# A graph layer with top-p attention: one guard less, and the finished tile's root moved behind the guess's chain on GpSimd

## The chip, the cores and the metric

The kernel runs on one core of a Trainium2 chip. Its time is in device microseconds, the median of several runs; of the kernel before, three runs gave 1342.86, 1344.52 and 1345.33 us. A profile is one execution more, taken with the hardware profiler; its rows have times from the start of the span. TensorE appears in it as PE (matmuls and transposes) and PEld (weight loads), VectorE as DVE, ScalarE as ACT, GpSimd as POOL, SyncE (which issues most DMAs) as SP.

## The reference

3327 nodes with 256 features, a sparse weighted adjacency `S`, and two steps of a mix of diffusion and attention. All is float32.

```python
h = relu(layernorm(x))                       # X of the layer
R = S + eye; R = R / R.sum(-1)               # diffusion
for n in range(2):
    q = Xa @ W1.T @ W2.T; k = Xa @ W3.T      # 64 wide
    probs = softmax(q @ k.T)                 # 3327 x 3327
    # top-p: keep the largest probabilities until their sum reaches 0.9, drop the rest
    A = probs * mask; A = A / max(A.sum(-1), 1e-12)
    Xf = R @ Xf
    Xa = A @ Xa
    Z = Z + Xf @ U1[n].T + Xa @ U2[n].T
out = x + (layernorm(h + Z) * ln_g + ln_b)
```

The sort of the reference is not done. Of each row only one number is wanted: the smallest probability that is kept.

## The kernel before, in words

Rows are tiled by 128: 26 tiles (`NT`), the last one partly filled, and 3328 columns (`NP`). The program makes two passes over the tiles, **step 0** (about the first 740 us) and **step 1** (the rest). In each, a tile goes through the same stations, spread over neighbouring iterations of one loop:

- `weights`: TensorE makes the logits `q @ k.T` in four pieces (`pl`, L597), ScalarE takes their exponentials into the row block `e` (L601; the last piece L607 and L609), with their sum `Z`.
- `measured`: a guess at the threshold. ScalarE computes a first guess from moments of the logits, and two or three times runs over the whole 128 x 3328 block (L632) to sum or count what lies below a guess; between these passes stand chains of operations on one column (128 x 1), the columns of the small tile `g`. They are done on ScalarE, VectorE and GpSimd. In step 1 (`measured_twice`) the last of these chains is the one the change touches: VectorE makes the mass below the second guess (L698, L699) and a slope (L705, L706); ScalarE takes logarithms (L701 to L703); GpSimd makes the exponent (L707 to L711); ScalarE's L713 turns it into the guess proper, `col(16)`. The passes read the block, the columns come from their sums `oa`.
- `settle`: VectorE keeps the elements below the guess (L728, 128 x 3328), takes the 8 largest of each of 20 segments (L733), of these the 32 or 40 largest (L740, L742), finds among them the exact threshold, and masks the row block with it (L762, 128 x 3328; L759 for the first and the last tile, in two pieces).
- `Sums`: TensorE transposes the masked block (`pt`, L808), ScalarE copies the transposes out (`eT`, L810), and TensorE sums `A @ X` (`pa`, L822).
- `spread`: diffusion by gathering rows (L899, L920: indirect DMAs that GpSimd issues) and small matmuls (`pr`, L928).
- `finish` (step 1): L958 adds attention and diffusion, L461 and L462 take mean and variance, `inverse` on GpSimd makes 1/sqrt of the variance, the **root** (L468 adds the epsilon, L469 is the power), L966 makes minus mean times root, and L973 to L976 scale, shift and add the input rows `xr`, all on GpSimd.

At the end a proof checks that every row's threshold was among the candidates. If one row fails, a second, complete program (`search_graph_layer`) runs behind the first. **Guards** protect the guess: where it cannot be trusted, a huge number is added, so that all elements become candidates. One guard goes by count (fewer than some 15 or 30 elements lie above), one by mass (too little lies below).

The order of work is written out by hand. An iteration has seven parts, and a table (`PLAN`, L1141; `OPEN` and `LAST` for the first and last iterations of step 1) names for each part the stations that take one stride, letter by letter: `m` measured, `w` weights, `d` settle, `s` spread, `f` finish, `g` one gather, `c` and `n` the rest of the last iteration's settle and measured. Each engine's queue then stands in the order of this text. In iteration i, `m` works for tile i + 1, and `f` for a tile that was finished in part 3. So on GpSimd, in step 1, between the third and the last part stand: four gathers, L688 to L691 (columns of the second guess), the root of the finished tile with L966, the chain L696 to L711, one gather; then L675 to L677 of the next tile.

Of the kernel before, what the change touches and what calls it, by code (L numbers as in the profile page):

```python
# [9 lines left out]
F32 = mybir.dt.float32  # L10
# [4 lines left out]
ALU = mybir.AluOpType  # L15
# [3 lines left out]
P = 128  # L19
# [4 lines left out]
NP = NT * P  # L24
# [288 lines left out]
BIG = 1.0e30  # L313
LNBIG = 69.0
# [31 lines left out]
def guess_graph_layer(ctx, tc, x, adj, w1t, w2t, w3t, u1t, u2t, ln_g, ln_b, out, flag):  # L346
# [9 lines left out]
    small = ctx.enter_context(tc.tile_pool(name="small", bufs=4))  # L356
# [5 lines left out]
    V, G, S, PE = nc.vector, nc.gpsimd, nc.scalar, nc.tensor  # L362
# [264 lines left out]
    def con(k):  # L627
        return one[:, k : k + 1]
# [5 lines left out]
    def measured_once(r):  # L634
        e, ms = r["e"], r["ms"]


        col = guessed(r, small.tile([P, 17], F32, tag="g", name="g"), 0)
        S.activation(col(4), col(2), AF.Square, bias=con(4))
        S.activation(col(11), col(4), AF.Identity, scale=ms(5), bias=ms(6))  # L640
        S.activation(col(1), col(0), AF.Exp, scale=-1.0, bias=con(5))
        G.tensor_scalar(col(7), col(9), 0.5, None, ALU.mult)
        G.tensor_scalar(col(8), col(9), 0.5 * NP, None, ALU.mult)
        G.tensor_scalar(col(5), col(1), OFFSET[0], None, ALU.mult)
        G.tensor_scalar(col(10), col(9), col(5), 1.0, ALU.mult, ALU.add)
        yield
        oa = small.tile([P, 3], F32, tag="oa", name="oa")
        through(e, AF.Relu, col(9), -1.0, oa[:, 0:1])
        yield
        through(e, AF.Sign, col(9), -1.0, oa[:, 1:2])  # L650
        yield
        S.activation(col(3), oa[:, 0:1], AF.Identity, scale=-1.0, bias=col(8))
        S.activation(col(4), oa[:, 1:2], AF.Relu, scale=col(7), bias=col(3))
        S.activation(col(6), col(4), AF.Ln, scale=col(1), bias=con(2))
        S.activation(col(3), col(4), AF.Square, scale=col(1), bias=con(1))
        S.activation(col(3), col(3), AF.Ln, scale=0.5, bias=col(10))
        S.activation(col(3), col(3), AF.Identity, scale=-1.0, bias=col(6))
        S.activation(col(3), col(3), AF.Exp, scale=col(11))
        yield

        V.tensor_scalar(col(5), oa[:, 1:2], NP - 31.0, BIG, ALU.is_gt, ALU.mult)
        V.tensor_scalar(col(6), col(4), col(1), 0.35, ALU.mult, ALU.is_lt)
        V.scalar_tensor_tensor(col(5), col(6), BIG, col(5), ALU.mult, ALU.add)
        V.tensor_scalar(col(3), col(3), 1.0e20, col(9), ALU.min, ALU.mult)
        V.tensor_tensor(col(16), col(3), col(5), ALU.add)

    def measured_twice(r):
# [4 lines left out]
        col = guessed(r, small.tile([P, 18], F32, tag="g", name="g"), 1)  # L672
# [6 lines left out]
        oa = small.tile([P, 3], F32, tag="oa", name="oa")  # L679
# [13 lines left out]
        through(e, AF.Sign, col(13), -1.0, oa[:, 2:3])  # L693
        yield
        d1 = col(17)
        G.tensor_scalar(col(0), oa[:, 2:3], NP - 61.0, BIG, ALU.is_gt, ALU.mult)  # L696
        G.tensor_scalar(col(0), r["Z"], 0.035, col(0), ALU.mult, ALU.add)
        V.tensor_scalar(col(15), oa[:, 2:3], oa[:, 1:2], col(14), ALU.subtract, ALU.mult)  # L698
        V.tensor_scalar(d1, col(15), col(4), 0.0, ALU.add, ALU.max)  # L699

# [3 lines left out]

        V.tensor_scalar(col(12), col(4), d1, 1.0e-30, ALU.subtract, ALU.add)  # L705
        V.reciprocal(col(12), col(12))  # L706
        G.tensor_scalar(col(12), col(12), col(8), 0.85, ALU.mult, ALU.max)  # L707
        G.tensor_scalar(col(11), col(12), 1.2, col(11), ALU.min, ALU.mult)
        G.tensor_tensor(col(2), col(3), col(2), ALU.subtract)
        G.tensor_scalar(col(15), d1, col(0), LNBIG, ALU.is_lt, ALU.mult)  # L710
        G.tensor_tensor(col(6), col(6), col(15), ALU.add)  # L711
        yield
        S.activation(col(16), col(2), AF.Exp, scale=col(11), bias=col(6))  # L713
        yield
# [242 lines left out]
    def finish(t, y, pa, ra):  # L957
        V.scalar_tensor_tensor(y, pa, ra, y, ALU.mult, ALU.add)  # L958
        yield
        mv = spread_of(y)  # L960
        yield
        xr = row.tile([P, D], F32, tag="xr", name="xr", bufs=1)
        nc.sync.dma_start(xr, x[t * P : (t + 1) * P])
        rstd = inverse(mv)
        nm = small.tile([P, 1], F32, tag="nm", name="nm")
        G.tensor_scalar(nm, mv[:, 0:1], rstd, -1.0, ALU.mult, ALU.mult)  # L966
        yield
        if t == NT - 1:
            G.tensor_tensor(xr, xr, bet, ALU.add)
            V.scalar_tensor_tensor(y, y, mv[:, 0:1], gam, ALU.subtract, ALU.mult)  # L970
            V.scalar_tensor_tensor(y, y, rstd, xr, ALU.mult, ALU.add)
        else:
            G.tensor_scalar(y, y, rstd, nm, ALU.mult, ALU.add)  # L973
            G.tensor_tensor(y, y, gam, ALU.mult)
            G.tensor_tensor(xr, xr, bet, ALU.add)
            G.tensor_tensor(y, y, xr, ALU.add)  # L976
        h = min(P, N - t * P)
        nc.sync.dma_start(out[t * P : t * P + h], y[:h])
# [152 lines left out]
    def refetch(t):  # L1131
# [7 lines left out]


    PLAN = (("gmdsssa", "gmcdsssa", "edawwpg", "gmsdga", "gmspdea", "ohgdawwqg", "gehmgq"),  # L1141
            ("llcmss", "lnms", "lwwnfd", "lcmdsssgggg", "fdsmwqdf", "llmdf", "lmwdg"))

    LAST = {NT - 1: ("cfss", "cn", "nd", "sss", "fddddddsf", "f", ""), NT: ("c", "", "", "ff", "ff", "fv", "f"),
            NT + 1: ("fv", "f", "", "", "f", "f", "f")}
# [142 lines left out]
```

## Time and profile before

| | us |
|---|---|
| median of three runs | 1344.52 |
| profiled execution | 1346.05 |
| its span, first to last instruction | 1344.3 |
| TensorE busy in the span | 1259.3 (94%) |
| VectorE busy | 1151.8 (86%) |
| ScalarE busy | 1074.2 (80%) |
| GpSimd busy | 1017.4 (76%) |

The page has one row of tenths per engine for forty slices of the span. Step 0 fills slices 3 to 21, step 1 slices 23 to 40. A share over the whole span mixes two stages with different limits, so the prediction reads them apart. A row of the order of time gives start, duration, engine, line, operation, what it writes and reads, its shape, and in brackets how long its engine was idle just before and who ended that.

### The profile page before, as it was taken

The page shows a single profiled execution, that of the slowest core. Times are in us where ns is not written, and L with a number is a line of the kernel's source. Part 1 is how long each engine was busy: PE and PEld are TensorE (multiplying, and loading weights), DVE is VectorE, ACT ScalarE, POOL GpSimd, SP SyncE. Part 2 cuts the span into 40 slices and gives each one's busy share as a digit, 9 for nine tenths or more (in the row PEclk, how much of TensorE's full clock was granted, in tenths as well). Part 3 has the DMA queues.
Part 4 walks back from the last instruction along what each step waited for, and adds up shares of the span by engine and source line. Part 5 has one row for each costly group of instructions (what it writes and reads, how often), then busy time and mean ns, then how long its engine had stood idle before and what let it go on. Part 6 is the DMA issues. An engine that isn't in the chain of part 4 may idle for free.

```text
span 1344.3 us, 22106 instructions
## 1 busy us (share of the span) xinstructions
PE 1259.3 (94%) x6396; PEld 956.0 (71%) x6396; DVE 1151.8 (86%) x3481; ACT 1074.2 (80%) x2315; POOL 1017.4 (76%) x1411
## 2 busy tenths in 40 slices
PE   5989899999999999999999589999999999999985
PEld 4535677778777787777777367777777777777774
DVE  6876899999999999999981698888998898988993
ACT  5476798888878888888853889899998999999951
POOL 6214888888888888887883587888888888888852
PEclk9999999999999999999999789999999999999998
DMA  7744455454555555455433213132222223131200
GB/s 265 254 132 133 123 153 160 141 157 136 144 157 145 154 142 155 137 152 154 117 103 91 79 50 90 54 95 62 86 79 69 87 65 95 53 95 61 82 24 23
DMA packets 100723, 153.13 MB, mean 114 GB/s; under 512 B 16849, under 2 KB 67152, under 8 KB 100592
## 3 DMA queue, kind: packets, MB, share of 16 engines
q1 hardware_dynamic: 83056, 108.72, 25.5%
q0 software_dynamic: 16640, 42.69, 12.7%
q8 instruction: 53, 0.87, 0.3%
q14 instruction: 78, 0.64, 0.2%
q10 hardware_dynamic: 896, 0.21, 0.1%
HBM read 120.88 MB, written 27.28 MB: 110 GB/s over the span
## 4 chain that ended last, share of the span: by engine, by line
PE 52%; ACT 25%; POOL 10%; DVE 7%; issue 3%; DMA 0%; SPq 0%; DVEq 0%; POOLq 0%; ACTq 0%
PE pa L822 23%; ACT ja L632 14%; PE pl L597 7%; PE pt L808 6%; PE pr L928 5%; PE pz L947 3%; PE pz L1016 3%; POOL g L710 3%; ACT eT L810 3%; ACT e L601 2%; POOL xg L920 2%; DVE cand L733 1%; ACT x L601 1%; DVE bb L740 1%; POOL g L707 1%
## 5 line engine op out<-in xcount | busy, mean ns | idle before, releaser
L822 PE MATMUL pa<-xw,eT 128*128 128x256 f32 x1352 | 323.7, 384 | 4.0 <-DVE s L958 3.8
L632 ACT ACTIVATE ja<-e,g 128x3328 uint8<-128x3328 f32 x106 | 325.7, 3073 | 0.1
L822 PE MATMUL pa<-x,eT 128*128 128x256 f32 x1352 | 322.0, 379 | 0.0
L822 PEld LDWEIGHTS pa<-xw,eT 128*128 128x128 f32 x1352 | 250.7, 190 | 64.0 <-issue 20.9
L822 PEld LDWEIGHTS pa<-x,eT 128*128 128x128 f32 x1352 | 242.8, 190 | 25.5
L733 DVE MAX8 cand<-w 128x8 f32<-128x168 f32 (+1 forms) x1040 | 253.4, 317 | 0.0
L810 ACT COPY eT<-pt 128x512 f32<-128x512 f32 (+1 forms) x364 | 198.4, 553 | 45.4 <-PE pt L808 39.1
L899 POOL DMA_INDIRECT ac<-in_adj,index x130 | 188.2, 1448 | 60.1 <-issue 26.5
L920 POOL DMA_INDIRECT xg<-bx,index x130 | 184.4, 1419 | 48.6 <-issue 16.2
L808 PE MATMUL pt<-ident,e 128*128 128x128 f32 x1144 | 176.0, 276 | 17.1 <-DVE e L759 8.5
L920 POOL DMA_INDIRECT xg<-vx,index x130 | 164.3, 1264 | 34.0 <-issue 32.9
L808 PEld LDWEIGHTS pt<-ident,e 128*128 128x128 f32 x1144 | 138.8, 143 | 71.0 <-issue 44.1
L728 DVE SCALAR_TENSOR_TENSOR w<-e,g 128x3328 f32<-128x3328 f32 x44 | 164.4, 3737 | 9.1 <-ACT g L713 8.2
L928 PE MATMUL pr<-xg,ac 128*128 128x257 f32 (+1 forms) x520 | 141.5, 396 | 10.4 <-DVE s L1124 7.0
L762 DVE SCALAR_TENSOR_TENSOR e<-e,rec 128x3328 f32<-128x3328 f32 x40 | 147.2, 3680 | 0.6
L601 ACT ACTIVATE e<-pl 128x832 f32<-128x832 f32 x132 | 113.9, 865 | 27.7 <-PE pl L597 24.5
L928 PEld LDWEIGHTS pr<-xg,ac 128*128 128x128 f32 x520 | 93.8, 194 | 37.5 <-issue 14.6
L597 PE MATMUL pl<-both,qT 64*128 64x416 f32 x416 | 100.0, 545 | 7.7 <-ACT e L601 4.3
L597 PE MATMUL pl<-after,qT 64*128 64x416 f32 x416 | 95.9, 555 | 1.8 <-ACT e L601 1.4
L852 DVE TENSOR_REDUCE fm<-at 128x4 f32<-128x512 f32 (+1 forms) x133 | 84.3, 634 | 0.0
L740 DVE MAX8 bb<-cand 128x8 f32<-128x160 f32 x234 | 75.6, 323 | 4.6
L632 ACT ACTIVATE ja<-x,g 128x3328 uint8<-128x3328 f32 x24 | 73.7, 3069 | 0.0
(261 smaller groups left out, 2045.3 us busy)
## 6 DMA issues: line engine op xcount, KB each, us to landing
at<-in_adj SPq DMA_DIRECT2D x114, 256.0 KB
cx<-ac SPq DMA_DIRECT2D x26, 384.0 KB
ac<-cx SPq DMA_DIRECT2D x26, 384.0 KB
wide<-in_adj SPq DMA_DIRECT2D x8, 832.0 KB
e<-in_adj SPq DMA_DIRECT2D x6, 832.0 KB
own<-bx SPq DMA_DIRECT2D x26, 128.5 KB
x<-in_x SPq DMA_DIRECT2D x13, 256.0 KB
qT<-both SPq DMA_DIRECT2D x104, 32.0 KB
```

What stands on the lines that cost most here:

```text
L597: PE.matmul(pl[:, a, :wd], qT[p, :], keys_of(step, a).rearrange("p a b -> p (a b)")[:, c : c + wd], start=True, stop=True)
L601: S.activation(e.rearrange("p (a n) -> p a n", a=2)[:, :, c : c + wd], pl[:, :, :wd], AF.Exp, accum_out=za[:, n : n + 1])
L632: S.activation(ja, e, f, bias=guess, scale=sign, accum_out=total)
L728: V.scalar_tensor_tensor(w, e, col(16), e, ALU.is_lt, ALU.mult, accum_out=d2)
L733: V.max(cand[:, 8 * s : 8 * s + 8], w[:, s * SEG : min(NP, (s + 1) * SEG)])
L762: V.scalar_tensor_tensor(e, e, at(1), e, ALU.is_ge, ALU.mult, accum_out=ra)
L808: PE.transpose(pt[:, j, :], e[:, (j0 + j) * P : (j0 + j + 1) * P], ident)
L810: S.copy(eT[:, :w, :], pt[:, :w, :])
L822: PE.matmul(self.pa, eT[:, c - 4 * k, :], self.xa[:, j, :], start=c == 0, stop=c == NT - 1)
L899: G.indirect_dma_start(out=ac[:, k, :], out_offset=None, in_=rows, in_offset=bass.IndirectOffsetOnAxis(ap=index[:, t, k : k + 1], axis=0), ...
L920: G.indirect_dma_start(out=xg[:, k, :w], out_offset=None, in_=rows, in_offset=bass.IndirectOffsetOnAxis(ap=index[:, t, k : k + 1], axis=0))
L928: PE.matmul(pr[:, :w], ac[:, k, :], own if k == KT - 1 else xg[:, k, :w], start=k == 0, stop=k == KT - 1)
```

## The change

Four edits.

1. In step 0 the guard by mass goes: two VectorE instructions a tile (L662, L663).
2. In step 1 the guard by mass goes too. Two GpSimd operations ahead of the chain (L696, L697) and two at its end (L710, L711) go; the guard by count is now added to the exponent's shift `col(6)` by two operations that stand between VectorE's L706 and L707, and need neither L706 nor ScalarE's logarithms.
3. In `finish` L966 goes; the scaling subtracts the mean and multiplies by the root in one instruction of the same shape.
4. In the table of step 1, part 4 and part 6 run `w` before `m` (logits' exponential before the guess's), and the third stride of `f` (the root, and the load of `xr`) moves from the end of part 5 to part 6, behind `m`. `OPEN` and `LAST` stay.

```diff
@@ measured_once @@
         V.tensor_scalar(col(5), oa[:, 1:2], NP - 31.0, BIG, ALU.is_gt, ALU.mult)
-        V.tensor_scalar(col(6), col(4), col(1), 0.35, ALU.mult, ALU.is_lt)
-        V.scalar_tensor_tensor(col(5), col(6), BIG, col(5), ALU.mult, ALU.add)
         V.tensor_scalar(col(3), col(3), 1.0e20, col(9), ALU.min, ALU.mult)
@@ measured_twice @@
         d1 = col(17)
-        G.tensor_scalar(col(0), oa[:, 2:3], NP - 61.0, BIG, ALU.is_gt, ALU.mult)
-        G.tensor_scalar(col(0), r["Z"], 0.035, col(0), ALU.mult, ALU.add)
...
         V.reciprocal(col(12), col(12))
+        G.tensor_scalar(col(0), oa[:, 2:3], NP - 61.0, LNBIG, ALU.is_gt, ALU.mult)
+        G.tensor_tensor(col(6), col(6), col(0), ALU.add)
         G.tensor_scalar(col(12), col(12), col(8), 0.85, ALU.mult, ALU.max)
         G.tensor_scalar(col(11), col(12), 1.2, col(11), ALU.min, ALU.mult)
         G.tensor_tensor(col(2), col(3), col(2), ALU.subtract)
-        G.tensor_scalar(col(15), d1, col(0), LNBIG, ALU.is_lt, ALU.mult)
-        G.tensor_tensor(col(6), col(6), col(15), ALU.add)
         yield
         S.activation(col(16), col(2), AF.Exp, scale=col(11), bias=col(6))
@@ finish @@
         rstd = inverse(mv)
-        nm = small.tile([P, 1], F32, tag="nm", name="nm")
-        G.tensor_scalar(nm, mv[:, 0:1], rstd, -1.0, ALU.mult, ALU.mult)
...
-            G.tensor_scalar(y, y, rstd, nm, ALU.mult, ALU.add)
+            G.tensor_scalar(y, y, mv[:, 0:1], rstd, ALU.subtract, ALU.mult)
@@ PLAN, step 1 @@
-            ("llcmss", "lnms", "lwwnfd", "lcmdsssgggg", "fdsmwqdf", "llmdf", "lmwdg"))
+            ("llcmss", "lnms", "lwwnfd", "lcmdsssgggg", "fdswmqdf", "llmd", "lwmfdg"))
```

GpSimd's queue in a middle tile of step 1, from the second guess's columns to the gather of part 6 (`g` is the tile of columns, `oa` the sums of the passes, `mv` mean and variance, `rstd` the root). Before:

```order
L691 TENSOR_SCALAR g<-g 128x1
L468 TENSOR_SCALAR rstd<-mv 128x1
L469 TENSOR_TENSOR rstd<-rstd,half 128x1
L966 TENSOR_SCALAR nm<-mv,rstd 128x1
L696 TENSOR_SCALAR g<-oa 128x1
L697 TENSOR_SCALAR g<-rec,g 128x1
L707 TENSOR_SCALAR g<-g 128x1
L708 TENSOR_SCALAR g<-g 128x1
L709 TENSOR_TENSOR g<-g 128x1
L710 TENSOR_SCALAR g<-g 128x1
L711 TENSOR_TENSOR g<-g 128x1
L920 DMA xg<-vx,index 128x256
```

And now; line numbers are those of the changed kernel, in which L705, L706 and L707 are the former L707, L708 and L709:

```order
L689 TENSOR_SCALAR g<-g 128x1
L703 TENSOR_SCALAR g<-oa 128x1
L704 TENSOR_TENSOR g<-g 128x1
L705 TENSOR_SCALAR g<-g 128x1
L706 TENSOR_SCALAR g<-g 128x1
L707 TENSOR_TENSOR g<-g 128x1
L468 TENSOR_SCALAR rstd<-mv 128x1
L469 TENSOR_TENSOR rstd<-rstd,half 128x1
L916 DMA xg<-vx,index 128x256
```

The root has moved from before the chain to behind it, ahead of the gather; three instructions a tile are gone.

ScalarE's queue in the same tile, from the pass over the block in part 3 to part 6 (`eT` are copies of transposes, `e` the row block, `za` the sums). Before:

```order
L810 COPY eT<-pt 128x512
L686 ACTIVATE g<-g,one 128x1
L687 ACTIVATE g<-g 128x1
L601 ACTIVATE e_99,za<-pl 128x2x416
L810 COPY eT<-pt 128x512
L632 ACTIVATE ja,oa<-e_102,g 128x3328
L810 COPY eT<-pt 128x512
L701 ACTIVATE g<-g,one 128x1
L702 ACTIVATE g<-g 128x1
L703 ACTIVATE g<-g,one 128x1
L607 ACTIVATE e_99,za<-pl 128x2x415
L609 ACTIVATE e_99,za<-pl 128x1
```

And now (L684 and L685 are the former L686 and L687; L697 to L699 the former L701 to L703; L806 the former L810):

```order
L806 COPY eT<-pt 128x512
L601 ACTIVATE e_99,za<-pl 128x2x416
L684 ACTIVATE g<-g,one 128x1
L685 ACTIVATE g<-g 128x1
L806 COPY eT<-pt 128x512
L632 ACTIVATE ja,oa<-e_102,g 128x3328
L806 COPY eT<-pt 128x512
L607 ACTIVATE e_99,za<-pl 128x2x415
L609 ACTIVATE e_99,za<-pl 128x1
L697 ACTIVATE g<-g,one 128x1
L698 ACTIVATE g<-g 128x1
L699 ACTIVATE g<-g,one 128x1
```

In part 4 the exponential of the third piece of logits, in part 6 that of the last piece (L607, L609) come before the guess's columns. The queues of TensorE and SyncE keep their order.

## The prediction

> **What bounds the kernel now.** I read the page first, then the busy times by stretch, then who waits for whom, then the order of time in two neighbouring tiles.
>
> From the page, the span and TensorE's busy tenths:
>
> ```profile
> span 1344.3 us, 22106 instructions
> ...
> PE   5989899999999999999999589999999999999985
> ```
>
> From the busy times by stretch (PE, PEld, DVE, ACT, POOL, then clock, DMA share, GB/s): 200 us of step 0, then two neighbouring tiles of step 1.
>
> ```profile
> 300.00:500.00 200.00, 199.88 (x1057) 155.62 (x1056) 189.38 (x574) 167.04 (x415) 167.69 (x192) 1.00 0.52 147
> ...
> 1039.59:1061.89 22.30, 21.19 (x110) 16.31 (x109) 20.64 (x59) 19.95 (x39) 19.77 (x26) 1.00 0.25 75
> 1061.89:1082.43 20.54, 20.48 (x106) 15.76 (x104) 17.96 (x54) 19.87 (x39) 17.74 (x27) 1.00 0.25 80
> ```
>
> Step 0 is TensorE's: 199.88 of 200 us. Step 1 alternates: a tile of 22.30 us, one of 20.54. ScalarE does the same work in both, so the long one holds a wait. From the waits of step 1 (us in total, times, longest):
>
> ```profile
> ACT g L713 <- POOL g L711: 21.6, 12, 2.6
> ...
> DVE w L728 <- ACT g L713: 9.8, 12, 1.7
> ...
> ACT g L701 <- DVE g L699: 6.6, 22, 1.8
> ```
>
> Twelve tiles hold 21.6 us of ScalarE waiting at L713 (the guess's last exponential) for GpSimd's L711. In order of time, a long tile:
>
> ```profile
> 1054.85 0.24 POOL L468 TENSOR_SCALAR rstd<-mv 128x1 f32<-128x1 f32 x1
> ...
> 1055.18 0.58 POOL L469 TENSOR_TENSOR rstd<-rstd,half 128x1 f32<-128x1 f32 x1
> ...
> 1055.48 0.16 DVE L706 RECIPROCAL g<-g 128x1 f32<-128x1 f32 x1
> ...
> 1055.86 0.26 POOL L966 TENSOR_SCALAR nm<-mv,rstd 128x1 f32<-128x1 f32 x1
> ...
> 1057.64 0.20 POOL L709 TENSOR_TENSOR g<-g 128x1 f32<-128x1 f32 x1
> ...
> 1057.73 3.69 DVE L762 SCALAR_TENSOR_TENSOR e<-e,rec 128x3328 f32<-128x3328 f32 x1
> ...
> 1057.92 3.67 POOL L710 TENSOR_SCALAR g<-g 128x1 f32<-128x1 f32 x1
> ...
> 1061.89 0.39 ACT L713 ACTIVATE g<-g 128x1 f32<-128x1 f32 x1 [1.69 <-POOL g L711]
> ```
>
> VectorE's mask L762 starts at 1057.73. GpSimd's L710, begun 0.19 us later, takes 3.67 us instead of some 0.3 and ends when the mask does. I call that caught. L709, begun 0.09 before the mask, took 0.20: what has begun is let through. In the short tile:
>
> ```profile
> 1075.91 0.34 POOL L691 TENSOR_SCALAR g<-g 128x1 f32<-128x1 f32 x1
> ...
> 1077.55 0.39 ACT L701 ACTIVATE g<-g,one 128x1 f32<-128x1 f32 x1 [0.19 <-DVE g L699]
> ...
> 1077.80 0.16 DVE L706 RECIPROCAL g<-g 128x1 f32<-128x1 f32 x1
> ...
> 1078.23 0.37 ACT L703 ACTIVATE g<-g,one 128x1 f32<-128x1 f32 x1
> ...
> 1078.51 0.84 ACT L607 ACTIVATE x<-pl 128x830 f32<-128x830 f32 x1
> ...
> 1079.34 0.15 ACT L609 ACTIVATE x<-pl 128x1 f32<-128x1 f32 x1
> ...
> 1080.02 3.69 DVE L762 SCALAR_TENSOR_TENSOR e<-e,rec 128x3328 f32<-128x3328 f32 x1
> ...
> 1080.13 4.56 POOL L920 DMA_INDIRECT xg<-vx,index  x1 [0.16 <-issue]
> ...
> 1082.43 0.39 ACT L713 ACTIVATE g<-g 128x1 f32<-128x1 f32 x1
> ```
>
> Here the chain ended before the mask, a gather that nobody waits for was caught instead, and L713 did not wait. In both tiles the mask starts 2.2 us after L706 (1055.48 to 1057.73, 1077.80 to 1080.02): that is the deadline.
>
> What would hold next is TensorE. Its first transposes of each tile, and the masks they wait for (count, least/median/greatest ns, first and last start; then who waited):
>
> ```profile
> 801.57 1.06 PE L808 MATMUL pt<-ident,e 128*128 128x128 f32 x8
> ...
> 1041.04 1.06 PE L808 MATMUL pt<-ident,e 128*128 128x128 f32 x8 [1.11 <-DVE e L762]
> ...
> 1061.71 1.04 PE L808 MATMUL pt<-ident,e 128*128 128x128 f32 x8
> ...
> 1083.86 1.06 PE L808 MATMUL pt<-ident,e 128*128 128x128 f32 x8 [1.19 <-DVE e L762]
> ...
> 1275.88 1.04 PE L808 MATMUL pt<-ident,x 128*128 128x128 f32 x8
> ```
>
> ```profile
> L762 DVE SCALAR_TENSOR_TENSOR e<-e,rec x15: 3685/3685/3686, 797.7 to 1229.1; 128x3328 f32<-128x3328 f32 x15
> ...
> L762 DVE SCALAR_TENSOR_TENSOR x<-x,rec x8: 3685/3685/3686, 863.4 to 1271.9; 128x3328 f32<-128x3328 f32 x8
> ...
>   PE pt L808: 13.8, 12
> ```
>
> From 1041.04 to 1061.71 TensorE ran a tile without a marked wait: 20.67 us. The next took 22.15, of which 1.19 is marked. Twenty-three masks make 22 tiles from 801.57 to 1275.88: 474.3 us, 21.56 each.
>
> **The change part by part.**
>
> Step 0 loses two VectorE instructions a tile (former L662, L663):
>
> ```profile
> L663 DVE SCALAR_TENSOR_TENSOR g<-g 128x1 f32<-128x1 f32 x24 | 6.6, 277 | 0.8
> ...
> L662 DVE TENSOR_SCALAR g<-g 128x1 f32<-128x1 f32 x24 | 4.8, 200 | 0.0
> ```
>
> That is 0.48 us a tile, 12.4 in all, hidden behind TensorE (199.88 of 200): I take 0. Without that cover it would be a gain of 12.4. Their results are not missed: by the kernel's own formulas on the reference's inputs, the mass guard fires in three rows of step 0, in all of which the count guard fires too, and in none of step 1.
>
> Step 1, the guess's chain on GpSimd. Behind L706 stood five instructions, now three; the count guard and the shift stand ahead and need only the third count. L468, L469 and L966, 1.27 us with their gaps (1054.85 to 1056.12), no longer stand ahead. In the long tile L710 began 0.19 us too late, with L711 still behind it; now L709 is the last, and would begin at 1057.64 - 1.27 = 1056.4, 1.3 us ahead of the mask.
>
> ScalarE's order cuts into this. In parts 4 and 6 the logits' exponential now comes before the guess's. L607 and L609 take 0.99 us, of which 0.19 fill the wait at L701 and 0.10 overlap (L607 starts 0.09 before L703 ends), so L703 ends 0.70 later against L706: at 1078.60 + 0.70 = 1079.30 in the short tile's time. The last subtraction (L709) waits for it and starts, at my estimate, 0.1 behind (between L709 and L710, on one engine, the gap is 0.08): at 1079.40, 0.6 ahead of the mask. The chain gets through, and L713 finds its operands ready. ScalarE also loses the wait at L701 (6.6 over 22): 0.3 us a tile, so 20.54 becomes 20.2.
>
> So ScalarE at 20.2 is faster than TensorE at 20.67, and TensorE sets the tile: 22 times 20.67 is 454.7 instead of 474.3, **minus 19.6**. What is late next is ScalarE, waiting for logits or transposes.
>
> The root now stands behind the chain: 0.28 after L709 comes L468 (the step from L709 to L710), 0.33 later L469: 1079.68 and 1080.01, with the mask at 1080.02. Whether the root is caught is a coin's toss. If not, the gather is, as in today's short tile: 0. If so, the gather goes under the next long VectorE instruction (L728) and GpSimd starts the next tile some 1.3 us later (a free gather takes 1.02, the row at 1005.75 below, and its gap); it has about 1 us to spare (from L691's end at 1076.25 to L706's at 1077.96, less two short operations), so 0.3 in 22 tiles, 6.6 at most. The next tile's chain, being late, ends nearer the mask, which then slides too; I take **plus 0.5**. Nobody else waits for the root before the next part 2.
>
> The Trainium skill ("SBUF — State Buffer", Who interferes with whom) has a rule against this placing: of a GpSimd operation and a VectorE one with two inputs in SBUF, whichever starts first blocks the other for its whole length. By it a root begun just ahead would push the mask back by up to 0.5 us a tile. The trace agrees on L710, but not on the reverse: L709 ran into the mask, and all 23 masks took 3.685 to 3.686 us. The sum goes by the rows.
>
> SP's and TensorE's queues keep their order.
>
> Four smaller terms:
>
> ```profile
> 760.10 0.30 POOL L710 TENSOR_SCALAR g<-g 128x1 f32<-128x1 f32 x1
> 760.48 0.19 POOL L711 TENSOR_TENSOR g<-g 128x1 f32<-128x1 f32 x1
> ...
> 840.18 3.77 POOL L707 TENSOR_SCALAR g<-g 128x1 f32<-128x1 f32 x1
> ...
> 1005.75 1.02 POOL L920 DMA_INDIRECT xg<-vx,index  x1 [2.62 <-issue]
> ...
> 1333.58 0.26 POOL L966 TENSOR_SCALAR nm<-mv,rstd 128x1 f32<-128x1 f32 x1
> ```
>
> In the first tile, which all wait for, L710 and L711 fall away: minus 0.6. The first tiles keep the table in which the root stands ahead; there L707 was caught by 0.01 us, and the new chain's third operation would still be: plus 1.3 (half of the longest wait, 2.6). The gather that waited 2.62 us for issue, once, will again: 0 to 2.6, plus 0.5, since ScalarE and VectorE then lead TensorE. At the end L966 is gone (minus 0.2), and VectorE starts the last long tile's L728 sooner (9.8 over 12, minus 0.8).
>
> Sum: -19.6 + 0.5 - 0.6 + 1.3 + 0.5 - 1.0 = **-18.9** on the span of 1344.3. The profiled execution took 1346.05 us, 1.5 more than the median 1344.52; on the median, **1325.6**.
>
> **Rivals.**
>
> *Half the catches stay* (0.12). GpSimd comes late to every second tile, because a caught gather or root pushes it back, and the last subtraction is caught. For it: margins are tenths. Against: the chain starts 1.35 us earlier. A pair of 42.84 then loses only ScalarE's waits at L701 (0.6) and L711 behind the release (0.2): 0.8 in 11 pairs, 8.8, with the first tile 9.4: 1335.
>
> *TensorE is no floor* (0.06). The Trainium skill ("Perfetto Trace Analysis", Identifying the Most-Contended Engine) holds matmul busy time a bad measure and weight-load occupancy a good one; here that is 15.76 of 20.54. As a mechanism: TensorE closes up and ScalarE's 20.2 sets the tile, 444.4 for 22, 10 us less: 1315. Against: the 20.67 without a marked wait.
>
> *Slower: caught in every tile* (0.06). At L607, now ahead of L701, ScalarE waits for TensorE's logits, which is likelier once TensorE is the bound. From 0.6 us of such waiting the last subtraction begins behind the mask in each tile, not in each second one. L713 then waits some 1.6 us on ScalarE's 20.2: 21.8 in 22 tiles is 479.6, plus 5.3: with the first tile 1349. Against: the waits of step 1 name no ScalarE wait for logits.
>
> *The change does not do what it says* (0.06). Either the wait only moves (L713 gets another releaser as late; 1344, 0.04), or rows fail the proof without the guard and the full search runs behind the program, at a price that no trace here shows (0.02).
>
> **How the numbers follow.** The forecast has 0.70, with 1321 to 1332 for itself (TensorE exactly at its floor and no smaller loss; a caught root in every tile). The range 1319 to 1337 takes in the first rival and leaves out the others, 0.18. About 0.2% is what a measurement can tell here: faster 0.70 + 0.12 + 0.06 and a little of the rest, 0.89; the same 0.04; slower 0.07.
>
> **What would show it.** The wait of L713 for GpSimd falls from 12 times to one or two; masks stand 20.6 to 20.7 us apart; TensorE no longer waits for L762 but from the first tiles; ScalarE begins to wait for logits or transposes. L469 takes 0.58 (let through) or near 4 us (caught). Masks 20.2 apart speak for the second rival, 21.8 and L713 waiting in each tile for the third; alternating tiles for the first. Step 0 must end when it did. The forecast is wrong if TensorE's tile takes more than 20.67 although it waits for nothing.

## The result, and the profile after

The changed kernel takes **1324.29 us** (1322.95 to 1326.55, four runs), the kernel before, on the same chip, 1344.92 (1342.86 to 1347.49, four): a ratio of 0.984, with a 95% interval of 0.9819 to 0.9861. The forecast was 1325.6 in 1319 to 1337. The profiled execution took 1324.6 us, its span 1322.9, against 1346.05 and 1344.3 before: 21.4 us less of span.

From the page of the changed kernel, the span, the busy times, and the engines' shares of the chain that ended last:

```profile
span 1322.9 us, 21977 instructions
...
PE 1254.3 (95%) x6396; PEld 956.6 (72%) x6396; DVE 1139.4 (86%) x3429; ACT 1073.5 (81%) x2315; POOL 994.1 (75%) x1333
...
PE 81%; DVE 8%; ACT 6%; POOL 2%; issue 2%; DMA 1%; SPq 0%; POOLq 0%; ACTq 0%; DVEq 0%
```

The same last line of the kernel before:

```profile
PE 52%; ACT 25%; POOL 10%; DVE 7%; issue 3%; DMA 0%; SPq 0%; DVEq 0%; POOLq 0%; ACTq 0%
```

TensorE now holds the chain in 81% of the span instead of 52%; ScalarE's share has fallen from 25% to 6%, GpSimd's from 10% to 2%. The waits of step 1 (770 to 1270 us here, 770 to 1290 in the prediction):

```profile
DVE s L954 <- PE pa L818: 13.1, 19, 0.9
...
ACT e L601 <- PE pl L597: 3.0, 10, 0.3
ACT g L709 <- POOL g L707: 2.0, 1, 2.0
...
DVE w L724 <- ACT g L709: 1.0, 1, 1.0
```

L709 is the former L713. Its 21.6 us of waiting in twelve tiles have become 2.0 in one, and VectorE's wait for it 1.0 instead of 9.8. In their place others wait for TensorE: VectorE for the finished sums, ScalarE for the logits. Two of the changed kernel's tiles by stretch, columns as in the prediction (busy PE, PEld, DVE, ACT, POOL):

```profile
1026.65:1047.01 20.36, 20.36 (x106) 15.85 (x105) 19.18 (x56) 19.71 (x39) 17.91 (x24) 1.00 0.27 82
1149.83:1170.47 20.64, 20.64 (x108) 16.08 (x107) 19.07 (x56) 19.89 (x39) 18.11 (x24) 1.00 0.28 81
```

The long and the short tile are gone, and TensorE is busy throughout. Its first transposes of the first and the last full tile:

```profile
801.34 0.49 PE L804 MATMUL pt<-ident,e 128*128 128x128 f32 x3
...
1257.93 0.49 PE L804 MATMUL pt<-ident,x 128*128 128x128 f32 x3
```

Twenty-two tiles in 456.6 us, 474.3 before. Twenty take 20.64 to 20.68 us, one 21.67 and one 21.90. What a GpSimd tile looks like now (GpSimd and VectorE's mask, in order of time):

```profile
1002.95 0.26 POOL L686 TENSOR_SCALAR g<-g 128x1 f32<-128x1 f32 x1
...
1005.64 0.20 POOL L707 TENSOR_TENSOR g<-g 128x1 f32<-128x1 f32 x1
...
1006.23 0.58 POOL L469 TENSOR_TENSOR rstd<-rstd,half 128x1 f32<-128x1 f32 x1
1006.28 3.69 DVE L758 SCALAR_TENSOR_TENSOR x<-x,rec 128x3328 f32<-128x3328 f32 x1
...
1007.01 3.96 POOL L916 DMA_INDIRECT xg<-vx,index  x1 [0.19 <-issue]
...
1011.02 2.95 POOL L673 TENSOR_SCALAR g<-g,law 128x1 f32<-128x1 f32 x1
...
1014.68 1.25 POOL L967 TENSOR_SCALAR s<-s,mv,rstd 128x256 f32<-128x256 f32 x1
...
1023.32 0.26 POOL L686 TENSOR_SCALAR g<-g 128x1 f32<-128x1 f32 x1
```

The chain's last operation (L707) is through 0.4 us ahead of the mask, the root's power (L469) starts 0.05 ahead of it and is let through, and the gather is caught. Two things here were not in the prediction. The scaling (L967) takes 1.25 us. And from one L686 to the next GpSimd goes from operation to operation with no pause over 0.3 us: 20.37 us.

### The profile page after: what moved, and what is told of

Same layout as the page of the kernel before. It is cut to its first block, busy times and chain, and to the rows that moved or that the text cites. A ratio compares the mean times of both kernels' runs of the same rounds, so it can differ in the third digit from the quotient of the medians.

```text
span 1322.9 us, 21977 instructions
## 1 busy us (share of the span) xinstructions
PE 1254.3 (95%) x6396; PEld 956.6 (72%) x6396; DVE 1139.4 (86%) x3429; ACT 1073.5 (81%) x2315; POOL 994.1 (75%) x1333
## 4 chain that ended last, share of the span: by engine, by line
PE 81%; DVE 8%; ACT 6%; POOL 2%; issue 2%; DMA 1%; SPq 0%; POOLq 0%; ACTq 0%; DVEq 0%
PE pa L818 39%; PE pl L597 12%; PE pt L804 10%; PE pr L924 9%; PE pz L943 3%; ACT ja L632 3%; PE pz L1010 2%; DVE cand L729 2%; PE pk L488 1%; DVE x L758 1%; DVE w L724 1%; PE pk L1054 1%; DVE cand L738 1%; DVE bb L736 1%; PE pb L870 1%
## 5 line engine op out<-in xcount | busy, mean ns | idle before, releaser
L806 ACT COPY eT<-pt 128x512 f32<-128x512 f32 (+1 forms) x364 | 198.2, 552 | 46.1 <-PE pt L804 38.0
L895 POOL DMA_INDIRECT ac<-in_adj,index x130 | 182.7, 1405 | 62.2 <-issue 28.1
L916 POOL DMA_INDIRECT xg<-bx,index x130 | 178.7, 1374 | 50.0 <-issue 15.4
L916 POOL DMA_INDIRECT xg<-vx,index x130 | 189.2, 1456 | 34.6 <-issue 33.2
L724 DVE SCALAR_TENSOR_TENSOR w<-e,g 128x3328 f32<-128x3328 f32 x44 | 162.6, 3694 | 2.3 <-ACT g L709 1.4
```

What stands on the lines that cost most here:

```text
L724: V.scalar_tensor_tensor(w, e, col(16), e, ALU.is_lt, ALU.mult, accum_out=d2)
L806: S.copy(eT[:, :w, :], pt[:, :w, :])
L895: G.indirect_dma_start(out=ac[:, k, :], out_offset=None, in_=rows, in_offset=bass.IndirectOffsetOnAxis(ap=index[:, t, k : k + 1], axis=0), ...
L916: G.indirect_dma_start(out=xg[:, k, :w], out_offset=None, in_=rows, in_offset=bass.IndirectOffsetOnAxis(ap=index[:, t, k : k + 1], axis=0))
```

## The experiments

"Step 1" below is the time from the start of step 1's first mask to the last instruction of the profiled execution: 566.5 us in the kernel before, 545.8 in the changed one. It leaves out step 0, whose length differs by up to 5 us between executions, and it comes from one execution of each kernel. Times are medians, each against the kernel before on the same chip.

| kernel | time, us | ratio to before (95%) | step 1, us |
|---|---|---|---|
| changed | 1324.3 | 0.984 (0.9819 to 0.9861) | 545.8 |
| root alone | 1353.7 | 1.006 (1.0036 to 1.0083) | 573.6 |
| root put back | 1337.2 | 0.992 (0.9892 to 0.9948) | 556.9 |
| guards alone | 1335.1 | 0.9907 (0.9883 to 0.9932) | 555.0 |
| swap alone | 1347.3 | 0.9994 (0.998 to 1.0008) | 564.4 |
| less TensorE | 1321.0 | 0.9815 (0.9791 to 0.9838) | 542.6 |
| no swap | 1327.4 | 0.9872 (0.9845 to 0.9898) | 546.7 |
| more GpSimd | 1336.6 | 0.9936 (0.9918 to 0.9953) | 556.6 |
| less GpSimd | 1333.3 | 0.9922 (0.9896 to 0.9948) | 550.7 |
| opening tile's root | 1324.7 | 0.9824 (0.9804 to 0.9844) | 545.1 |
| step 0's guard back | 1325.8 | 0.9838 (0.982 to 0.9856) | 545.6 |
| shift computed late | 1326.4 | 0.9841 (0.9825 to 0.9858) | 545.1 |
| other operations | 1324.7 | 0.9832 (0.9807 to 0.9857) | 544.7 |

### The parts, one by one

**Root alone**: the kernel before, with the root behind the chain.

```diff
-  "fdsmwqdf", "llmdf", "lmwdg"
+  "fdsmwqdf", "llmd", "lmwfdg"
```

> The kernel before, with one edit: in step 1's table the third stride of f (root, L966, load of xr) moves from part 5 to part 6 behind m. All guards and L966 stay, ScalarE's order stays. Theory (a GpSimd operation that begins behind the mask L762 is caught until the mask ends, and only a catch of the guess's chain costs time): the chain of five begins 1.27 us earlier, L711 starts at about t + 1.6 (t is the start of L706) and is free of the mask at t + 2.23; but the root then starts at t + 2.0 and its power at t + 2.3 and is caught, L966 and the gather go under the next long VectorE instruction, GpSimd comes some 1.6 us late into the next tile, and there L711 ends within tenths of the mask. So part of the gain: tiles alternate between 20.6 and about 21.7, 1330 to 1340 us. Rival (the root's place is what did it, the guards are decoration): the whole gain, 1324 to 1327. Rival (the place does not matter, fewer instructions do): 1343 to 1346.

1353.7: slower. The expectation had the right event (the root is caught) and the wrong size. From the fifth mask to the last but one the masks stand 21.9 us apart, but for one interval of 24.35 at the gather that waits for issue. Two neighbouring tiles on GpSimd:

```profile
1061.25 3.63 POOL L711 TENSOR_TENSOR g<-g 128x1 f32<-128x1 f32 x1
...
1065.97 3.19 POOL L966 TENSOR_SCALAR nm<-mv,rstd 128x1 f32<-128x1 f32 x1
...
1070.52 0.33 POOL L675 TENSOR_SCALAR g<-g,law 128x1 f32<-128x1 f32 x1
...
1083.15 3.68 POOL L468 TENSOR_SCALAR rstd<-mv 128x1 f32<-128x1 f32 x1
1086.91 4.06 POOL L469 TENSOR_TENSOR rstd<-rstd,half 128x1 f32<-128x1 f32 x1
```

In the first the chain's last operation is caught under the mask, and L966 under L728 (the settle step's first pass, the second long VectorE instruction of a tile); in the second both halves of the root are caught, one under each. With the guards still in the chain the root comes too late, and it costs GpSimd more behind the mask than it did ahead of it.

**Root put back**: the changed kernel, with the root ahead of the chain again.

```diff
-  "fdswmqdf", "llmd", "lwmfdg"
+  "fdswmqdf", "llmdf", "lwmdg"
```

> The changed kernel with the root back in part 5, ahead of the chain; guards gone, w before m as in the change. Theory: the root's two operations take 0.99 us with gaps ahead of the chain, GpSimd still reaches the third operation of the chain before ScalarE's logarithm is done, it starts at about t + 1.6 against the mask at t + 2.23 and is not caught; TensorE keeps its 20.65 us a tile: 1324 to 1327, the same as the changed kernel. Rival (the root's place is what did it): catches in every second tile again, 1334 to 1344.

1337.2: with the guards gone and the logits first, the root's place is worth some 11 us (step 1: 556.9 against 545.8), which this expectation missed. The rival fits. Between 1030 and 1250 us:

```profile
ACT g L709 <- POOL g L707: 9.8, 5, 2.2
...
POOL g L673 <- ACT g L672: 3.0, 3, 1.2
```

Every second tile has its catch as in the kernel before.

**Guards alone**: the changed code with the whole former table.

```diff
-  "fdswmqdf", "llmd", "lwmfdg"
+  "fdsmwqdf", "llmdf", "lmwdg"
```

> The changed kernel with the whole table of before: guards by mass and L966 gone, shift ahead of the chain, but the root ahead of the chain and m before w. Theory: the chain's last operation waits for nothing late and starts at about t + 1.0 in a tile where GpSimd is on time and at most 0.3 later where it is not; no catch; ScalarE at 20.5 us a tile is still under TensorE's 20.65: 1324 to 1328. Rival (ScalarE's order is part of the gain): 20.65 is not reached, 1330 to 1336.

1335.1; missed too. The rival gave this range, but ScalarE's order is not the reason: the run without the swap, below, comes out at 1327.4. Tiles of 20.52, 20.53 and 21.9 us follow one another. In one of the three the gather begins ahead of the mask and is let through, and GpSimd then stands idle, for L673 needs what ScalarE has not yet made; its next operation is caught under L724:

```profile
1094.41 1.12 POOL L916 DMA_INDIRECT xg<-vx,index  x1 [0.16 <-issue]
1097.00 1.54 POOL L673 TENSOR_SCALAR g<-g,law 128x1 f32<-128x1 f32 x1 [1.47 <-ACT g L672]
1098.61 3.59 POOL L674 TENSOR_SCALAR g<-g 128x1 f32<-128x1 f32 x1
```

There GpSimd falls back by 0.4 us against the mask, in the next tile by 0.35 (the mask starts 4.28, 3.87 and 3.52 us behind L686), and in the third the chain is caught.

**Swap alone**: the kernel before with logits ahead of the guess in parts 4 and 6.

```diff
-  "fdsmwqdf", "llmdf", "lmwdg"
+  "fdswmqdf", "llmdf", "lwmdg"
```

> The kernel before with w ahead of m in parts 4 and 6 of step 1 and nothing else. Theory: ScalarE saves its short waits but its logarithm L703 ends 0.7 us later against L706, the chain's L709 starts at t + 1.6, L710 at t + 1.9 and L711 at t + 2.25, just behind the mask at t + 2.23: caught in every tile instead of every second, L713 waits near 1.9 us on ScalarE's 20.36: about 22.2 us a tile, 1350 to 1360. If L711 slips through in half of the tiles: 1338 to 1344. Rival (ScalarE's short waits are what bounded step 1): 0.3 us less in 22 tiles, 1336 to 1339.

1347.3, no difference, and in none of the expected ranges: the main expectation had forecast a slower kernel. Most of its tiles alternate between 22.62 and 20.01 us, 21.3 on average. It shows how sharp the edge of a catch is. L711 in two tiles, with its mask:

```profile
1056.82 3.69 DVE L762 SCALAR_TENSOR_TENSOR e<-e,rec 128x3328 f32<-128x3328 f32 x1
...
1061.30 0.19 POOL L711 TENSOR_TENSOR g<-g 128x1 f32<-128x1 f32 x1
...
1079.43 3.69 DVE L762 SCALAR_TENSOR_TENSOR e<-e,rec 128x3328 f32<-128x3328 f32 x1
1079.49 3.68 POOL L711 TENSOR_TENSOR g<-g 128x1 f32<-128x1 f32 x1
```

In the first L711 stands behind a caught operation and runs free after the mask. In the second it begins 0.06 us behind the mask's start and is caught; in other tiles of this run it begins 0.02 to 0.04 behind and takes 0.19.

**No swap**: the changed kernel without the exchange.

```diff
-  "fdswmqdf", "llmd", "lwmfdg"
+  "fdsmwqdf", "llmd", "lmwfdg"
```

> The changed kernel with the guess again ahead of the logits in parts 4 and 6; the root stays behind the chain and the guards stay away. Theory (the gain comes from GpSimd's shorter loop and the root's place; ScalarE's order only moves slack): 1322 to 1327 us, GpSimd's loop at most 20.65. Rival (ScalarE's wait at the log must go for the gain, and the earlier chain lets the gather slip ahead of the mask, so that GpSimd loses 1.5 us after it, as in the run without the guards alone): 1330 to 1337.

1327.4, 0.4 over the theory's range. Step 1 is 0.9 us longer than in the changed kernel, with masks 20.49 to 20.55 apart where TensorE doesn't hold them, instead of 20.36. The gather does not slip ahead of the mask, since the root stands in between. The swap is worth about 1 us.

By step 1 the parts alone give +7.1 (root), -11.5 (guards, with the folded shift) and -2.1 (swap), which sums to -6.5; together they give -20.7, and root and guards without the swap -19.8. Guards and root must come together.

### Who sets the tile

**More GpSimd**: two unused small operations in the middle of the last scaling.

```diff
             G.tensor_scalar(y, y, mv[:, 0:1], rstd, ALU.subtract, ALU.mult)
             G.tensor_tensor(y, y, gam, ALU.mult)
+            nm = small.tile([P, 1], F32, tag="nm", name="nm")
+            for _ in range(2):
+                G.tensor_scalar(nm, mv[:, 0:1], rstd, -1.0, ALU.mult, ALU.mult)
```

> The changed kernel with two more small GpSimd operations a tile (0.26 us each and 0.08 of gap, 0.68 in all) in the middle of the last scaling, far from the guess and the mask; their result is not used. Theory (GpSimd works without a pause; its loop of 20.36 becomes 21.04): masks 21.04 apart, 20 tiles 0.39 over TensorE's 20.65 and the lead that VectorE had, +8 to +10: 1332 to 1335 us. Rival of the prediction (GpSimd has about 1 us to spare in a tile): 1323 to 1326.

1336.6, a little over the theory's range, and 10.8 us more in step 1. GpSimd's first column of each tile between 862 and 990 us (count, least, median and greatest ns, first and last start), and who waited for it:

```profile
L686 POOL TENSOR_SCALAR g<-g x7: 272/278/283, 862.8 to 989.0; 128x1 f32<-128x1 f32 x7
...
  DVE g L694: 4.8, 4
```

Six tiles in 126.2 us: 21.03 each, and the masks stand 21.03 to 21.05 apart. Every operation that GpSimd gets shows in full; there is no spare time in its tile. In four tiles of this stretch VectorE's L694, with which the chain ahead of the mask begins, has a marked wait for it, 4.8 us in all.

**Less GpSimd**: the kernel before without the addition of the bias.

```diff
-            G.tensor_tensor(xr, xr, bet, ALU.add)
             G.tensor_tensor(y, y, xr, ALU.add)
```

> The kernel before, with its guards, order and root, but without the GpSimd addition of the layer norm's bias to the residual in step 1 (0.73 us and its gap a tile; the output lacks the bias). Theory (GpSimd's loop without a pause, 21.41 us on average in the kernel before, is what set its tiles): the loop falls by some 0.75 to about 20.65, 1326 to 1333 us, although guess, guards and order are untouched. Rival of the prediction (the last operation of the guess's chain is caught in each second tile because of what stands ahead of it, and GpSimd is only late by the caught operations): the long and short tiles stay, 1342 to 1346.

1333.3, just above the theory's range, and 15.8 us less of step 1. Neither guess, guards nor order is touched, and yet the long tiles go: masks stand 20.51 apart, then 20.65. The waits between 1060 and 1250 us, first of this run, then of the kernel before:

```profile
POOL g L675 <- ACT g L674: 12.9, 9, 1.5
POOL xg L920 <- issue: 11.8, 47, 0.3
ACT g L701 <- DVE g L699: 1.7, 9, 0.2
```

```profile
POOL xg L920 <- issue: 11.0, 44, 0.3
ACT g L713 <- POOL g L711: 8.4, 5, 1.7
```

With 0.7 us less to do GpSimd waits for ScalarE in each tile; in the kernel before GpSimd has no wait but the gaps of its gathers' issue, and ScalarE waits for it. From there too, its first column between 1030 and 1250 us:

```profile
L688 POOL TENSOR_SCALAR g<-g x11: 267/277/279, 1032.2 to 1246.4; 128x1 f32<-128x1 f32 x11
```

Ten tiles in 214.2 us: 21.42. That is the mean of its long and short tiles. So in step 1 the kernel before was bound by GpSimd.

**Less TensorE**: the changed kernel without two of 26 chunks of the sum in step 1.

```diff
             for c in range(4 * k, min(4 * k + 4, NT)):
+                if self.step and c in (9, 13):
+                    continue
```

> Leaves out two of the 26 chunks of the sum over rows in step 1 (so that sum is incomplete); all else is the changed kernel. In the changed kernel GpSimd's loop from tile to tile takes 20.36 us without a pause in tiles 6 to 8 and 13 to 16, and the masks follow it; from tile 9 and from tile 17 on they stand 20.65 apart. Theory (TensorE holds the 20.65, GpSimd's loop is next at 20.36): the masks stand 20.36 apart in all tiles but the one with the gather's stall; some 12 tiles gain 0.29 each, 1319 to 1322 us. Rival of the prediction (ScalarE is next at 20.2): masks 20.2 apart, 1316 to 1319. Rival (TensorE was no bound): masks 20.65 as before, 1323 to 1326.

1321.0, within the expected range; the time alone is not clear of the changed kernel's (the intervals of the two ratios overlap), but the masks are. From 1028.4 to 1211.7 us the masks stand 20.36 to 20.38 apart:

```profile
L758 DVE SCALAR_TENSOR_TENSOR e<-e,rec x8: 3683/3685/3686, 1028.4 to 1211.7; 128x3328 f32<-128x3328 f32 x8
```

Nine tiles in 183.3 us, 20.37 each (the e blocks are two thirds of them). TensorE did hold the 20.65, and the next bound is GpSimd at 20.36, not ScalarE at 20.2.

### The folded shift, and two small parts

**Shift computed late**: the fold undone, with the shift's operation ahead of the scaling.

```diff
-            G.tensor_scalar(y, y, mv[:, 0:1], rstd, ALU.subtract, ALU.mult)
+            nm = small.tile([P, 1], F32, tag="nm", name="nm")
+            G.tensor_scalar(nm, mv[:, 0:1], rstd, -1.0, ALU.mult, ALU.mult)
+            G.tensor_scalar(y, y, rstd, nm, ALU.mult, ALU.add)
```

> The changed kernel with the folded shift undone: the scaling takes root and shift again (0.56 us in the kernel before, 1.25 in the changed one), and the shift's own operation stands directly ahead of it, far from the mask. Theory (of GpSimd's tile some 14.75 us are its work and 5.6 are lost behind the two long VectorE instructions; the fold itself costs 0.70 and saves 0.36): the loop goes from 20.36 to about 20.0, the masks stand 20.0 apart where TensorE does not hold them to 20.65, and the time falls by 0 to 2, since TensorE sets nearly all tiles already: 1322 to 1324.5 us. Rival (the scaling takes 1.25 us for another reason than its operations or operands): loop 20.7, 1324 to 1327.

**Other operations**: the same two operands, multiplied and added.

```diff
-            G.tensor_scalar(y, y, mv[:, 0:1], rstd, ALU.subtract, ALU.mult)
+            G.tensor_scalar(y, y, mv[:, 0:1], rstd, ALU.mult, ALU.add)
```

> The changed kernel whose scaling multiplies and adds instead of subtracting and multiplying, with the same two operands (so the layer norm's output is another one); it tells why the scaling takes 1.25 us. If it is the pair of operations: 0.56 us, GpSimd's loop 19.7, and the masks of the early tiles show who is next: 20.2 if ScalarE as the prediction had it, 20.0 if as in the long-and-short runs; 1321 to 1324.5 us. If it is the mean's column being half of a pair: 1.25 us as in the changed kernel, loop 20.36, 1323 to 1326 us.

The scaling between 1030 and 1250 us, in the changed kernel, with the shift late, and with other operations:

```profile
L967 POOL TENSOR_SCALAR s<-s,mv,rstd x11: 1254/1255/1256, 1035.0 to 1240.8; 128x256 f32<-128x256 f32 x11
```

```profile
L969 POOL TENSOR_SCALAR s<-s,rstd,nm x11: 558/559/561, 1036.9 to 1242.9; 128x256 f32<-128x256 f32 x11
```

```profile
L967 POOL TENSOR_SCALAR s<-s,mv,rstd x11: 558/560/564, 1034.7 to 1241.2; 128x256 f32<-128x256 f32 x11
```

It is the pair of operations: subtract and multiply take 1.25 us, multiply and add 0.56, on the same operands. The fold saves one operation of 0.26 (0.36 with its gap) and costs 0.70. Undone, GpSimd's loop falls to 20.10 (expected: 20.0), and with the other operations to some 19.65 (expected: 19.7). The time does not follow: 1326.4 (above its range) and 1324.7 against the changed kernel's 1324.3, ratios to the kernel before of 0.9841, 0.9832 and 0.984; step 1 is 0.7 and 1.1 us shorter, less than a measurement of the whole tells. TensorE sets nearly all tiles, and the masks of both runs settle at 20.65. Right behind the gather's stall the second run has two masks 19.67 apart. That is one tile, in which ScalarE and VectorE may have used what they had done during the stall; no run shows that they can keep it up.

**Opening tile's root**: tile 3's table with the root behind the chain and the logits first.

```diff
-    OPEN[2] = OPEN[3] = OPEN[1]
+    OPEN[2] = OPEN[1]
+    OPEN[3] = ("cmss", "nms", "wwnfd", "cmdsssgggg", "fdswmqdf", "mgd", "mwfdg")
```

> The changed kernel in which tile 3 (the last of the hand-written opening tables) also has the root behind the chain and the logits ahead of the guess. Theory (the one chain that is still caught in the changed kernel, with a wait of 1.96 us at L709, is caught because the root stands ahead of it there): that wait goes, the mask of tile 4 follows 20.4 to 20.7 us behind that of tile 3 instead of 22.37, and the span falls by 1.0 to 1.7 us: 1322 to 1324 us by the times, which can hardly tell it, so the masks decide. Rival (that chain is late for another reason, the pauses in which GpSimd waits for VectorE's reciprocal at L705): the wait stays, 1324 to 1326.

1324.7; 0.7 us less of step 1. The next mask follows after 21.96 instead of 22.37: between the two expectations. The chain is earlier but still caught, now with its last operation, 0.2 us behind the mask's start; L709 waits 1.3 us instead of 2.0. So the root was a part of the cause, and the theory's size was wrong. The rival's reason does not hold either: in that tile GpSimd has no wait. What still stands ahead of the chain, by the opening table, is a gather, between L689 and L703:

```profile
837.62 0.99 POOL L916 DMA_INDIRECT xg<-vx,index  x1
...
840.00 3.53 POOL L707 TENSOR_TENSOR g<-g 128x1 f32<-128x1 f32 x1
```

Without its 0.99 us L707 would begin ahead of the mask (839.80); no run took it away.

**Step 0's guard back**: the former L662 and L663 in the changed kernel.

```diff
         V.tensor_scalar(col(5), oa[:, 1:2], NP - 31.0, BIG, ALU.is_gt, ALU.mult)
+        V.tensor_scalar(col(6), col(4), col(1), 0.35, ALU.mult, ALU.is_lt)
+        V.scalar_tensor_tensor(col(5), col(6), BIG, col(5), ALU.mult, ALU.add)
```

> The changed kernel with the two VectorE instructions of step 0's guard put back (0.48 us a tile, 12.4 us in all). Theory of the prediction (hidden behind TensorE): no change, 1322 to 1327 us. Rival (they stand on the path that sets step 0's tiles): up to 1336.

1325.8, no difference that the times can tell: the two instructions were hidden.

None of these variants that does the whole work is faster than the changed kernel by more than the times can tell.

## Why the prediction was right, and where its reasons were wrong

**Step 0 at nothing** was right (1325.8 with the instructions back).

**The chain gets through, and TensorE sets the tile** was right: 20.65 us forecast as 20.67, so 22 tiles give -20.0 for -19.6. By the Trainium skill ("Perfetto Trace Analysis", Identifying the Most-Contended Engine), which the rival without a floor rested on, weight-load occupancy tells more than matmul busy time. Here 16.08 of 20.64 us of weight load stood beside a full 20.64 of matmul, and with less for TensorE the tiles fell to 20.37: the measurement speaks for the busy time.

**The root as a coin's toss, +0.5**: nothing. It starts 0.05 us ahead of the mask in the tiles that GpSimd sets and some 0.2 ahead in those that TensorE sets, and was let through in all of these. There is order in that: where GpSimd is late, VectorE's L694 waits for L686, and in no tile of any run does the mask start less than 3.33 us behind L686 (1002.95 to 1006.28). The root's power stands 3.28 behind it.

The masks took 3.683 to 3.686 us with a root that runs up to 0.5 us into them. By the rule of the Trainium skill against this placing ("SBUF — State Buffer", Who interferes with whom), they should have waited or taken longer; the trace disagrees, as the prediction said. But the rule is not empty. Wider operations do lengthen the other long VectorE instruction. In the kernel before, in the tiles with a catch, a gather begins 0.29 us ahead of L728 and is let through:

```profile
1019.20 1.12 POOL L920 DMA_INDIRECT xg<-vx,index  x1 [0.17 <-issue]
...
1019.49 3.91 DVE L728 SCALAR_TENSOR_TENSOR w<-e,g 128x3328 f32<-128x3328 f32 x1 [1.65 <-ACT g L713]
```

In all twelve such tiles L728 took 3.83 to 3.91 us instead of 3.67. So what is let through is not always free.

**The opening tile's catch, +1.3**: +1.0 (the tile of 21.67). **The gather's wait for issue, +0.5**: it came back at the same gather and cost +1.25 (the tile of 21.90). **Fill, -0.6**: the first guess did come 0.64 sooner behind the start of step 1 (from L607 at 741.78 to L713 at 760.70, now from 741.65 to 759.93), but TensorE, still at the sums of the tile before, was not ready for its masks sooner, and its first transposes gained 0.2 (801.57 to 801.34).

**The end, -1.0**: this term was mis-sized; it measured -3.4 (from the last full tile's transposes to the end 68.4 us before, 65.0 now). The prediction took the average of a wait for the last tile. But the end hangs on VectorE: the chain that ended last runs on it alone from 1242.3 to 1281.3. Its last two masks start 19.7 us apart (1253.1 and 1272.7 below; 1271.9 and 1293.3 before: 21.4, the whole of a catch), and the first of them 4.9 ahead of TensorE's transposes (1253.1 to 1257.93) instead of 4.0:

```profile
L758 DVE SCALAR_TENSOR_TENSOR e<-e,rec x16: 3683/3685/3691, 797.0 to 1272.7; 128x3328 f32<-128x3328 f32 x16
...
L758 DVE SCALAR_TENSOR_TENSOR x<-x,rec x8: 3684/3685/3685, 860.5 to 1253.1; 128x3328 f32<-128x3328 f32 x8
```

The sum comes out as -20.0 + 1.0 + 1.25 - 0.2 - 3.4 = -21.4, the measured difference (the terms divide the span, so they must add up to it); by the forecast -18.9.

**What was wrong is the account of GpSimd.** "It has about 1 us to spare" and "what is late next is ScalarE" are refuted by the runs with more GpSimd and less TensorE. The spare time was read as GpSimd's wait for VectorE's reciprocal; but that chain on VectorE begins behind GpSimd's own first column, and now L689 ends at 1004.25, the reciprocal at 1004.21. GpSimd was the bound of the kernel before, and the catches of L711 were part of what filled its time. Its tile is work plus what it loses behind the two long VectorE instructions. Before, in the long tile from 1053.47 to 1074.94:

```profile
1053.47 0.27 POOL L688 TENSOR_SCALAR g<-g 128x1 f32<-128x1 f32 x1
...
1063.20 3.15 POOL L675 TENSOR_SCALAR g<-g,law 128x1 f32<-128x1 f32 x1
...
1074.94 0.28 POOL L688 TENSOR_SCALAR g<-g 128x1 f32<-128x1 f32 x1
...
1079.78 0.19 POOL L711 TENSOR_TENSOR g<-g 128x1 f32<-128x1 f32 x1
```

L710 loses 3.67 - 0.31 = 3.36, L675 3.15 - 0.33 = 2.82 (0.31 and 0.33 are what they take when let through): 21.47 - 6.18 leaves 15.29 us of work. The changed kernel loses 3.96 - 1.12 at the gather (1.12 is what it takes when let through) and 2.95 - 0.34 at L673: 20.37 - 5.45 leaves 14.92. So 0.37 of the gain is work (the guards' operations some 0.75 and L966 0.36 less, the scaling 0.70 more) and 0.73 is loss: the root runs through the mask's first 0.5 us, and a gather rather than the chain is caught. The run with the root alone loses 6.4 and 6.9 in turn, and its loops of 21.62 and 22.15 leave some 15.2 of work, close to the kernel before; with 0.68 more work, the run with more GpSimd gives 14.92 + 0.68 + 5.45 = 21.05 (measured 21.03).

**Why the chain is no longer caught.** The prediction put the last subtraction 0.6 us ahead of the mask, held back by ScalarE's logarithm. In the middle tiles it begins 0.64 to 0.91 ahead. In the tiles that TensorE sets the forecast path holds: L707 begins at 1149.02, 0.09 behind ScalarE's L699. In those that GpSimd sets it does not: L699 ends at 1025.23, L707 begins at 1026.00 by GpSimd's own queue, and the agreement of 0.64 with 0.6 is luck. There both L707 and the mask hang on GpSimd's first column.

The mask starts 3.33 us behind L686 (before: L688) or later. A chain whose last operation begins later than that gets through only while GpSimd leads, that is, while the mask is held by something else and starts still later; and GpSimd, being the bound, loses its lead until the chain is caught and the mask of the next tile delayed with it. In tiles without a catch the last operation began 4.84 us behind L688 in the kernel before (1074.94 to 1079.78), 3.45 with the root alone, 3.7 with the guards alone, 3.7 to 3.8 with the root put back, and 2.69 in the changed kernel (1002.95 to 1005.64). Only the last is under 3.33, which is why neither part works alone.

Two more runs bear it out. With more GpSimd, which then sets every tile, L707 begins 2.70 behind L686 (1096.62 to 1099.32) and behind the opening tiles no chain is caught. With less GpSimd the last operation begins 4.79 behind L688, but GpSimd leads (the mask starts 5.32 behind), and the chain is caught only in two opening tiles and in the tile of the gather's stall. That 3.33 us is the deadline was read from the traces; no run moved it by itself.

**The swap** was given a larger part than it has ("ScalarE also loses the wait at L701"): about 1 us, since GpSimd's 20.36 and TensorE's 20.65 are longer than the 20.2 that it was to bring.

## What to carry to other kernels

An engine that works without a pause can be the bound, even with the lowest busy share (GpSimd, 76%) and whatever the waits name: follow one of its instructions from tile to tile, look for idle time, and take some of its work away to see whether the tile shortens. Where an operation can be held up by another engine, count the hold as its owner's time, and put something there that nobody waits for and that is long enough to use the time; moving an operation into such a place pays only if all that stands ahead of it fits. Check the duration of an instruction whose operations change, even when its shape does not.

## What the runs showed of the hardware

- On GpSimd a 128 x 256 two-operation instruction with two columns as operands took 1.25 us for subtract and multiply and 0.56 for multiply and add.
- A GpSimd operation of one column that is under way when a long two-input VectorE instruction starts is let through, and lengthens it by 0.02 us at most (L728 3.69 instead of 3.67 with the root alone). Wider ones did lengthen it: L728 took 3.83 to 3.91 us behind a gather begun 0.29 us ahead, and 3.97 behind the 128 x 256 addition L975. Not always: the masks took 3.69 with a gather begun 0.21 ahead.
- The edge lies within 0.06 us behind the start, and not at one place: L711 was let through at 0.02 to 0.04 and held at 0.05 and 0.06 (the swap alone), L707 of the changed kernel's code was let through at 0.05 (the guards alone, at 1261.82), L707 of the kernel before was held at 0.01 (the prediction's row at 840.18). An operation let through behind the start lengthened the mask, by up to 0.035 us (3.72 at 1261.77 with the guards alone).
- An indirect gather is held in the same way: 3.93 to 4.57 us instead of 0.94 to 1.14.
- In each run one gather of step 1, always the same, waited 2.62 us for issue. Why is open.
